# Transposing normalised rows and folded weights by VectorE turns and a round trip through memory, instead of on TensorE

## The chip, the cores and the metric

The kernel runs on one core of a Trainium2 chip. The metric is the time on the device of one execution, in microseconds (us). Before the change it is 2511.91 us, the median of 3 runs (2510.31 to 2513.71). All arithmetic is in fp32, except two small masks in bf16.

A core has five engines with a queue of instructions each: TensorE (PE in the profile, with its weight loads as PEld), VectorE (DVE), ScalarE (ACT), GpSimd (POOL), and SyncE (SP), which here only issues transfers between the on-chip memory and the chip's large memory.

## The reference

Four blocks run one after the other on `x` of 8 batch entries, 256 rows and 128 columns, with a context of 64 rows and 64 columns for each entry. The third block is nearly all of the time: six layers, each with self-attention, cross-attention to the context, and a feed-forward part. Cut to what matters:

```python
def _ln(x, g, b, eps=1e-05):
    m = jnp.mean(x, axis=-1, keepdims=True)
    v = jnp.mean(jnp.square(x - m), axis=-1, keepdims=True)
    return (x - m) / jnp.sqrt(v + eps) * g + b

def _mha(s, t, kv_w, q_w, o_w, o_b, mask):        # 16 heads of 64
    k, v = jnp.split(s @ kv_w, 2, axis=-1)
    q = t @ q_w
    k, v, q = (_heads(k), _heads(v), _heads(q))
    scores = jnp.einsum('bhqd,bhkd->bhqk', q, k) * D ** (-0.5)
    scores = jnp.where(mask[:, None] == 0, jnp.float32(-1000000000.0), scores)
    attn = jax.nn.softmax(scores, axis=-1)
    o = jnp.einsum('bhqk,bhkd->bhqd', attn, v)
    return o.transpose(0, 2, 1, 3).reshape(t.shape[0], t.shape[1], H * D) @ o_w + o_b
# each of 6 layers, t of (8, 256, 128):
#   n = _ln(t, norm);  t = t + _mha(n, n, sa_kv, sa_q, sa_ow, sa_ob, mask of 256 x 256)
#   n = _ln(t, norm);  t = t + _mha(context, n, ca_kv, ca_q, ca_ow, ca_ob, mask of 64)
#   n = _ln(t, pre);   t = t + relu(n @ ff_w1 + ff_b1) @ ff_w2 + ff_b2
```

## The kernel before

The whole of `t` stays on the chip, 128 rows in a partition group, two groups (`QT`) for each batch entry. A matmul contracts over partitions, so each of the three normalisations of a layer needs its result turned: from rows in partitions (`xn`) to the 128 columns in partitions (`tT`). That is done 3 x 8 x 6 = 144 times in the layers, by `ahead`.

The order of all work is written out by hand. Every step of every entry is put at a tick and a phase (`at(tick, phase, fn)`), the steps are sorted by that pair, and at the end a loop chains each engine's instructions in that order. An engine named in the tuple `engines` therefore runs its instructions in exactly this order: PE, DVE, ACT and POOL before the change. SP isn't in the tuple, so that its transfers go out when the framework places them.

A layer runs in three stages. Self-attention (SA) has four ticks for each entry `b`, with `T = T0 + 4b`. Cross-attention (CA) has two ticks for each, feed-forward (FF) one. Preparations for an entry lie some ticks before its own, so that stages overlap at their edges.

What one tick of SA does, by phase: two groups of scores on PE (1.0 and 1.1); their maxima on DVE and their exponentials on ACT (`exps`, phases 2.0 and 2.1, lines 905 to 921, eight ACTIVATE instructions for a tick); the division on POOL and the 32x32 turns of the weights on DVE (2.2, 2.3, 8.0, 8.1); the weighted values on PE (3.0); then, from phase 3.5, the projections of a later entry. For entry `b` the first key and both query projections (`project`, line 855) stand at tick T - 4, phases 3.5 to 3.7, the second keys at T - 3, the values at T - 2 and T - 1. Tick T - 4 of entry `b` is the first tick of entry `b - 1`, so for `b` from 1 to 7 these projections follow the scores of entry `b - 1` on PE. Each projection is copied out of PSUM by ACT.

`ahead` (line 802) makes `tT` in four steps. `moments` (DVE) and `scales` (POOL) find mean and reciprocal deviation. `normal` makes `xn`, on DVE for SA and on ACT for CA and FF. `trans` (line 837) turns `xn` with two PE transposes into PSUM, and ACT copies it into `tT` with the gain and the bias of the normalisation (line 843). SA has `trans` at (T - 5, 7.2): on ACT that lies ahead of the exponentials of tick T - 4. FF has it at (T - 1, 2.9), ahead of the relus of the same tick.

`plan_ca_weights` (line 1005) folds the cross-attention's weights, once in a layer: `turned` makes two transposes of a 128 x 1024 matrix, eight PE transposes and one ACT copy each, and `folded` multiplies the results into `AT` and `WVO`.

FF is `first` (line 1094; eight matmul records, then four relus on ACT) at tick T, and `second` (sixteen matmul records) at T + 1.

Of the kernel before, what the change touches and what calls it, by code (L numbers as in the profile page):

```python
# [8 lines left out]
F32 = mybir.dt.float32  # L9
I32 = mybir.dt.int32  # L10
BF16 = mybir.dt.bfloat16
AF = mybir.ActivationFunctionType
# [15 lines left out]
def tile_xattn_stack(ctx: ExitStack, tc: tile.TileContext, io, out: bass.AP):  # L28
    nc = tc.nc
# [21 lines left out]
    def tp_tile():  # L51
        return one_bank("tp")
# [56 lines left out]
    ident = const.tile([P, P], F32, tag="ident", name="ident")  # L109
# [83 lines left out]
    W = {}  # L193

    def load_sa(l):
        sk = sb([D, H * HD], "w_sk", 1, wpool)
        nc.sync.dma_start(out=sk, in_=io["L2_sa_kv"][l][:, : H * HD])

        sv = sb([D, 4, 2, 2 * HD], "w_sv", 1, wpool)
        sv_v = io["L2_sa_kv"][l][:, H * HD :].rearrange("p (g a x) -> p a g x", g=2, a=4)  # L200
        for a in range(4):
            nc.sync.dma_start(out=sv[:, a], in_=sv_v[:, a])
        sq = sb([D, H * HD], "w_sq", 1, wpool)
        nc.sync.dma_start(out=sq, in_=io["L2_sa_q"][l])
        sow = sb([P, HC, D], "w_sow", 1, wpool)
# [3 lines left out]
        W["sa", l] = (sk, sv, sq, sow, ob)  # L209

    def load_ca(l):

        ckv = sb([P, H * HD], "w_ckv", 1, wpool)
        for i in range(2):
            nc.sync.dma_start(
                out=ckv[DM * i : DM * i + DM],
                in_=io["L2_ca_kv"][l][:, H * HD * i : H * HD * (i + 1)],
            )
        cq = sb([D, H * HD], "w_cq", 1, wpool)
        nc.sync.dma_start(out=cq, in_=io["L2_ca_q"][l])  # L220
        cow = sb([P, HC, D], "w_cow", 1, wpool)
# [3 lines left out]
        W["ca", l] = (ckv, cq, cow, ob)  # L225

    def load_ff(l):
        w1 = sb([D, FF], "w_f1", 1, wpool)
# [50 lines left out]
    def at(tick, phase, fn):  # L279
        plan.setdefault(tick, []).append((phase, fn))  # L280
# [521 lines left out]
    def ahead(b, stats_at, normal_at, tT_at, g, bias, st, on_scalar=True):  # L802

        def moments():
            st["mv"] = sm([P, QT, 2], "mv")
            for j in range(QT):
                six = sm([P, 6], "six")
                nc.vector.bn_stats(six, tt(b)[:, j, :])
                nc.vector.bn_aggr(st["mv"][:, j, :], six)

        def scales():
            mv = st["mv"]
            ve = sm([P, QT], "ve")
            nc.gpsimd.tensor_scalar(ve, mv[:, :, 1], 1e-5, None, ALU.add)
            st["rstd"] = sm([P, QT], "rstd")
            nc.gpsimd.tensor_tensor(st["rstd"], ve, mhalf, ALU.pow)  # L816
            if on_scalar:
                nm = sm([P, QT], "nm")
                nc.gpsimd.tensor_tensor(nm, mv[:, :, 0], st["rstd"], ALU.mult)
                st["nm"] = sm([P, QT], "nm2")  # L820
                nc.gpsimd.tensor_scalar(st["nm"], nm, -1.0, None, ALU.mult)

        def normal():
            st["xn"] = sb([P, QT, D], "xn", 3)
            for j in range(QT):
                if on_scalar:
                    nc.scalar.activation(
                        st["xn"][:, j, :], tt(b)[:, j, :], AF.Identity,
                        scale=st["rstd"][:, j : j + 1], bias=st["nm"][:, j : j + 1],
                    )  # L830
                else:
                    nc.vector.tensor_scalar(
                        st["xn"][:, j, :], tt(b)[:, j, :], st["mv"][:, j, 0:1],
                        st["rstd"][:, j : j + 1], ALU.subtract, ALU.mult,
                    )

        def trans():
            ps = tp_tile()
            xn = st.pop("xn")
            for j in range(QT):  # L840
                nc.tensor.transpose(ps[:, j * P : (j + 1) * P], xn[:, j, :], ident)
            st["tT"] = sb([D, S], "tT", 3)
            nc.scalar.activation(st["tT"], ps[:, :S], AF.Identity, scale=g, bias=bias)

        at(*stats_at, moments)
        at(stats_at[0], 8.4, scales)
        at(*normal_at, normal)
        at(*tT_at, trans)

    def plan_sa(l, b, T):  # L850
# [134 lines left out]
        def mask():  # L985
            st["nm"] = load_mask(b)

        ahead(b, (T - 6, 8.3), (T - 5, 2.6), (T - 5, 7.2), norm_g, norm_b, st, False)
        at(T - 2, -1, mask)
        at(T - 4, 3.6, lambda: project(W["sa", l][2], "q", HD ** -0.5, 0, False))  # L990
        at(T - 4, 3.7, lambda: project(W["sa", l][2], "q", HD ** -0.5, 1, False))
# [13 lines left out]
    def plan_ca_weights(l, T):  # L1005


        st = {}
        W["fold", l] = st

        def turned(name, w, scale):
            def fn():
                ps = two_banks("tp")
                for c in range(HC):
                    nc.tensor.transpose(
                        ps[:, c * P : (c + 1) * P], w()[:, c * P : (c + 1) * P], ident
                    )
                st[name] = big("o", shape=(P, HC, P))
                flat = st[name].rearrange("p c x -> p (c x)")
                if scale is None:  # L1020
                    nc.scalar.copy(flat, ps)
                else:
                    nc.scalar.mul(flat, ps, scale)
            return fn

        def folded(name, cols, w):
            def fn():
                tiles = [two_banks("mm").rearrange("p (c d) -> p c d", c=HC) for _ in range(2)]
                res = sb([P, HC, D], name, 1, heap)
                for c in range(HC):  # L1030
                    for r in range(2):
                        rows = slice(r * HD, (r + 1) * HD)
                        nc.tensor.matmul(
                            tiles[r][rows, c, :], lhsT=st["kvT"][rows, c, cols],
                            rhs=w()[rows, c, :], start=True, stop=True,
                        )
                for r in range(2):
                    rows = slice(r * HD, (r + 1) * HD)
                    nc.scalar.copy(res[rows], tiles[r][rows])  # L1039
                st[name] = res  # L1040
            return fn

        at(T, 3.6, turned("kvT", lambda: W["ca", l][0], None))
        at(T + 1, 3.6, turned("WqT", lambda: W["ca", l][1], HD ** -0.5))
        at(T + 2, 3.6, folded("AT", slice(0, DM), lambda: st["WqT"]))
        at(T + 3, 3.6, folded("WVO", slice(DM, 2 * DM), lambda: W["ca", l][2]))

    keys_of = {}

    def plan_ca(l, b, T):  # L1050
        st = {}
# [25 lines left out]
        def res():  # L1077
            st["tb"] = residual(b, W["ca", l][3])

        ahead(b, (T - 4, 6), (T - 3, 2.95), (T - 2, 2.9), norm_g, norm_b, st)  # L1080
        if b % 2 == 0:
            at(T - 2, 3.7, keys_both)
        at(T + 2, 3.2, make_values)
# [11 lines left out]
    def plan_ff(l, b, T):  # L1095
# [29 lines left out]
                tt(b), ps[:, :S].rearrange("p (a d) -> p a d", a=QT), st["tb"]  # L1125
            )

        ahead(b, (T - 3, 6), (T - 2, 3.3), (T - 1, 2.9), pre_g[:, l : l + 1], pre_b[:, l : l + 1], st)
        at(T, 3.1, first)
        at(T + 1, 3.2, second)  # L1130

# [61 lines left out]
            at(T + n, 4.5 - 0.1 * n, step)  # L1193


    at(0, -1, lambda: load_sa(0))
    at(8, -1, lambda: load_ca(0))
    at(8, -0.9, lambda: load_ff(0))
    plan_start()
    for b in range(B):  # L1200
# [3 lines left out]
    for l in range(NL):  # L1204
        T_ca = T0 + 4 * B
        T_ff = T_ca + 2 * B
        for b in range(B):
            plan_sa(l, b, T0 + 4 * b)
        plan_ca_weights(l, T_ca - 6)
        for b in range(B):  # L1210
            plan_ca(l, b, T_ca + 2 * b)
            plan_ff(l, b, T_ff + b)
        if l > 0:
            at(T0, -1, lambda l=l: load_ff(l))
        if l + 1 < NL:
# [8 lines left out]
    for b in range(B):  # L1224
# [76 lines left out]
```

## Time and profile before

| | us |
|---|---|
| median of the runs | 2511.91 |
| the profiled execution, its own time | 2511.47 |
| its span, first to last instruction | 2509.8 |
| around the span | 1.7 |
| mean granted TensorE clock | 0.977 |
| DVE busy | 1821.0 |
| ACT busy | 1738.0 |
| POOL busy | 1442.8 |
| one layer, from the first weighted values after the fold to the same in the next (762.37 to 1147.80) | 385.4 |

One layer of 385 us is repeated six times; the two small blocks ahead take some 160 us, the last block is short. Busy shares say little for a kernel with three stages, since each has its own limit. Two further readings matter here. An engine's row in the timeline merges instructions of one line and tile, and a remark in brackets gives the idle time before it and who ended it. And the mean clock below 1 comes from short stretches in which the TensorE clock was granted at one half.

### The profile page before, as it was taken

How to read it: one execution, taken by the hardware profiler on the slowest of the kernel's cores; microseconds unless marked ns; L12 is line 12 of the kernel's file. 1: busy time of each engine (PE TensorE's matmuls, PEld its weight loads, DVE VectorE, ACT ScalarE, POOL GpSimd, SP SyncE). 2: the span in 40 equal slices, each digit the busy share in tenths (PEclk: the TensorE clock that was granted, in tenths of full speed). 3: DMA queues.
4: the chain of work that ended last, by engine and by line, in shares of the span. 5: the costliest groups of instructions: out<-in, count | busy, mean ns of one | idle time of the engine just before them, and what ended most of it. 6: DMA issues, size and time to landing. Idle time of an engine off the chain costs nothing.

```text
span 2509.8 us, 100205 instructions
## 1 busy us (share of the span) xinstructions
PE 2393.4 (95%) x42507; PEld 1766.2 (70%) x42507; DVE 1821.0 (73%) x5976; ACT 1738.0 (69%) x4540; POOL 1442.8 (57%) x2477
## 2 busy tenths in 40 slices
PE   8999999999999999999999999989999989999996
PEld 4667777677777676777776777776777776777774
DVE  5768887738887738887738887747887746888764
ACT  5567777667777657777657777657777657778651
POOL 3745557825556835556845555854555854555763
PEclk9999999999999999999999999999999999999996
DMA  6000021000011000012000012001002000000000
GB/s 172 2 11 17 22 57 34 3 11 20 20 47 52 2 12 20 20 37 63 2 8 23 20 29 63 11 3 27 21 20 70 12 2 20 20 20 12 2 1 17
DMA packets 94770, 64.31 MB, mean 26 GB/s; under 512 B 7729, under 2 KB 90353, under 8 KB 94322
## 3 DMA queue, kind: packets, MB, share of 16 engines
q1 hardware_dynamic: 93730, 57.57, 8.4%
q8 instruction: 334, 5.47, 0.9%
q14 instruction: 114, 0.93, 0.1%
q10 hardware_dynamic: 592, 0.33, 0.1%
HBM read 55.78 MB, written 2.10 MB: 23 GB/s over the span
## 4 chain that ended last, share of the span: by engine, by line
PE 69%; POOL 13%; DVE 7%; ACT 7%; issue 3%; POOLq 0%; DVEq 0%; ACTq 0%
PE mm L953 14%; PE mm L861 13%; PE sc L898 12%; PE mm L971 7%; PE mm L880 7%; POOL e L360 6%; PE mm L1103 3%; PE mm L1120 3%; DVE m L359 3%; POOL e L372 3%; PE mm L388 2%; ACT e L357 2%; ACT e L917 2%; PE sc L341 1%; POOL rstd L816 1%
## 5 line engine op out<-in xcount | busy, mean ns | idle before, releaser
L927 POOL TENSOR_SCALAR e<-e,rs 128x256 f32<-128x256 f32 x1536 | 702.5, 478 | 693.0 <-DVE rs L925 684.4
L917 ACT ACTIVATE e<-e,mn 128x256 f32<-128x256 f32 x1536 | 758.3, 495 | 131.3 <-DVE mn L912 130.5
L912 DVE CUSTOM_DVE_ANT_0 e<-sc,nm 128x256 f32<-128x256 f32 x1536 | 542.8, 419 | 124.3 <-PE sc L898 124.1
L937 DVE STREAM_TRANSPOSE eTc<-e 128x512 f32<-128x512 f32 x768 | 519.7, 697 | 66.2 <-POOL e L927 64.6
L953 PE MATMUL mm<-eTc,v 32*64 32x256 f32 x12288 | 383.4, 387 | 18.4 <-ACT AT L1039 8.1
L898 PE MATMUL sc<-k,q 64*32 64x256 f32 x12288 | 378.9, 380 | 5.9 <-DVE mn L912 4.2
L953 PEld LDWEIGHTS mm<-eTc,v 32*64 32x64 f32 x12288 | 285.0, 135 | 113.7 <-issue 30.2
L898 PEld LDWEIGHTS sc<-k,q 64*32 64x32 f32 x12288 | 220.5, 106 | 125.0 <-issue 46.1
L360 POOL TENSOR_TENSOR e<-e,m 128x1024 f32<-128x1024 f32 x112 | 213.1, 1902 | 129.2 <-DVE m L359 129.1
L917 ACT ACTIVATION_READ_ACCUMULATOR e<-e,mn 128x1 f32 x1536 | 287.2, 187 | 0.0
L359 DVE TENSOR_REDUCE m<-sc 128x16 f32<-128x1024 f32 x112 | 137.1, 1224 | 165.5 <-ACT e L357 165.5
L388 PE MATMUL mm<-v,k 128*128 128x128 f32 x1792 | 235.8, 287 | 5.4 <-DVE k L380 4.9
L388 PEld LDWEIGHTS mm<-v,k 128*128 128x128 f32 x1792 | 219.2, 200 | 26.5 <-issue 10.4
L341 PE MATMUL sc<-q,tT 128*32 128x256 f32 x3072 | 217.1, 382 | 0.0
L372 POOL TENSOR_TENSOR e<-e,r 128x1024 f32<-128x1024 f32 x112 | 213.0, 1902 | 0.7 <-DVE r L371 0.7
L366 ACT ACTIVATE e<-e 128x1024 f32<-128x1024 f32 x112 | 119.0, 1063 | 115.7 <-POOL e L360 115.7
L286 ACT COPY v<-mm 128x1024 f32<-128x1024 f32 x96 | 97.2, 1012 | 134.2 <-PE mm L880 134.2
L861 PE MATMUL mm<-tT,w_sk 128*128 128x256 f32 x768 | 189.6, 390 | 0.0
L971 PEld LDWEIGHTS mm<-w_sow,o 128*128 128x128 f32 x1536 | 175.1, 192 | 17.7 <-issue 14.4
L880 PE MATMUL mm<-w_sv,tT 128*32 128x256 f32 x3072 | 185.7, 382 | 0.0
L971 PE MATMUL mm<-w_sow,o 128*128 128x128 f32 x1536 | 183.6, 278 | 1.5 <-ACT WVO L1039 1.5
L861 PE MATMUL mm<-tT,w_sq 128*128 128x256 f32 x768 | 173.6, 379 | 0.0
(212 smaller groups left out, 3521.0 us busy)
## 6 DMA issues: line engine op xcount, KB each, us to landing
nm<-mask_d SPq DMA_DIRECT2D x192, 128.0 KB, 2.9
w_sk<-in_L_sa_kv_dram SPq DMA_DIRECT2D x6, 512.0 KB, 4.1
w_sv<-in_L_sa_kv_dram SPq DMA_DIRECT2D x24, 128.0 KB, 2.4
w_sq<-in_L_sa_q_dram SPq DMA_DIRECT2D x6, 512.0 KB, 3.5
w_sow<-in_L_sa_ow_dram SPq DMA_DIRECT2D x6, 512.0 KB, 4.0
w_ckv<-in_L_ca_kv_dram SPq DMA_DIRECT2D x12, 256.0 KB, 4.9
w_cq<-in_L_ca_q_dram SPq DMA_DIRECT2D x6, 512.0 KB, 4.9
w_cow<-in_L_ca_ow_dram SPq DMA_DIRECT2D x6, 512.0 KB, 3.9
```

The lines of the kernel that those rows point to most:

```text
L360: nc.gpsimd.tensor_tensor(e, e, m.unsqueeze(2).to_broadcast([P, 16, M]), ALU.subtract)
L372: nc.gpsimd.tensor_tensor(tl["e"], tl["e"], r.unsqueeze(2).to_broadcast([P, 16, M]), ALU.mult)
L388: nc.tensor.matmul(ps[:, :D], lhsT=eT[:, s].rearrange("p q x -> p (q x)"), rhs=vw[:, r, k, g, :], start=(s == 0), stop=(s == 7),)
L861: nc.tensor.matmul(ps[:, i * S : (i + 1) * S], lhsT=w[:, c * P : (c + 1) * P], rhs=st["tT"], start=True, stop=True,)
L880: nc.tensor.matmul(ps[32 * a : 32 * a + 32, i, :], lhsT=st["tT"][:, kb * 32 : (kb + 1) * 32], rhs=sv[:, a].rearrange("p g x -> p (g x)"), ...
L898: nc.tensor.matmul(sc[32 * a : 32 * a + 32, r, j, :], lhsT=st["q"][g][rows, a, qb * 32 : (qb + 1) * 32], rhs=st["k"][g][rows, a, :], start ...
L912: nc.vector.tensor_tensor_reduce(e[:, i, :], sc4[:, i, :], st["nm"][:, 2 * jj + i % 2, :], -1.0, 3.0 * BIG, ALU.add, ALU.min, mn[:, i : i ...
L917: nc.scalar.activation(e[:, i, :], e[:, i, :], AF.Exp, scale=-1.0, bias=mn[:, i : i + 1], accum_out=rs[:, i : i + 1],)
L927: nc.gpsimd.tensor_scalar(e[:, i, :], e[:, i, :], rs[:, i : i + 1], 1.0, ALU.mult, ALU.mult)
L937: nc.vector.transpose(eT[:, r, :, 2 * jj : 2 * jj + 2, :], e[:, 2 * r : 2 * r + 2, :].rearrange("p j (k x) -> p k j x", x=32),)
L953: nc.tensor.matmul(ops[a // 2][r * HD : (r + 1) * HD, a % 2, :S], lhsT=st["v"][kb // 4][rows, kb % 4, (2 * g + r) * HD : (2 * g + r + 1) * ...
L971: nc.tensor.matmul(st["ps"][:, j * D : (j + 1) * D], lhsT=st["oT"][c // 4][:, c % 4, j * P : (j + 1) * P], rhs=sow[:, c, :], start=(c == 0 ...
```

## The change

Three things change together.

First, `ahead` no longer uses PE. After `normal`, a new step `blocks` turns 32x32 blocks on DVE, and four transfers write the four block columns to a buffer in the large memory (`zd`). One tick later `fetch` reads the buffer back, so that the 128 columns lie in partitions (`raw`). `trans` is now one ACT instruction, from `raw` to `tT`, with the gain and the bias.

Second, the steps move. SA's statistics and normalisation go two ticks earlier for `b > 0`, and `trans` moves from (T - 5, 7.2) to (T - 4, 2.15); for `b = 0` it moves to (T - 4, 3.45). FF's normalisation goes one tick earlier and its `trans` from (T - 1, 2.9) to (T, 2.15). CA's normalisation goes two ticks earlier, its `trans` stays at (T - 2, 2.9).

Third, the two weight transposes are made in the same way, in place, with a regrouping copy on POOL, and the scale of the queries moves into `folded`. SP joins the engines whose order is fixed, and the weight loads are issued in parts over several ticks (`load_sa` and `load_ca` become generators, with a `yield` after each part).

```diff
+        def blocks():
+            xn = st.pop("xn")
+            z = sb([P, 4, QT, 32], "z", 2)
+            nc.vector.transpose(z, xn.rearrange("p q (j x) -> p j q x", x=32))
+            zd = st["zd"] = dram.tile([4, 32, 4, QT * 32], F32, tag="zd", name=uniq("zd"), bufs=4)
+            for j in range(4):
+                nc.sync.dma_start(
+                    out=zd[j].rearrange("b i x -> i b x"), in_=z[:, j].rearrange("p q x -> p (q x)")
+                )
+
+        def fetch():
+            st["raw"] = sb([P, 4, QT, 32], "raw", 4)
+            nc.sync.dma_start(
+                out=st["raw"].rearrange("p i q x -> p (i q x)"),
+                in_=st.pop("zd").rearrange("j b i x -> (j b) (i x)"),
+            )
+
         def trans():
-            ps = tp_tile()
-            xn = st.pop("xn")
-            for j in range(QT):
-                nc.tensor.transpose(ps[:, j * P : (j + 1) * P], xn[:, j, :], ident)
             st["tT"] = sb([D, S], "tT", 3)
-            nc.scalar.activation(st["tT"], ps[:, :S], AF.Identity, scale=g, bias=bias)
+            nc.scalar.activation(
+                st["tT"].rearrange("p (q i x) -> p q i x", q=QT, i=4),
+                st.pop("raw").rearrange("p i q x -> p q i x"), AF.Identity, scale=g, bias=bias,
+            )
...
         at(*normal_at, normal)
+        at(normal_at[0], normal_at[1] + 0.01, blocks)
+        at(normal_at[0] + 1, 0, fetch)
         at(*tT_at, trans)
...
-        ahead(b, (T - 6, 8.3), (T - 5, 2.6), (T - 5, 7.2), norm_g, norm_b, st, False)
+        if b == 0:
+            ahead(
+                b, (T - 6, 8.3), (T - 5, 2.6), (T - 4, 3.45), norm_g, norm_b, st, False
+            )
+        else:
+            ahead(b, (T - 8, 8.3), (T - 7, 2.6), (T - 4, 2.15), norm_g, norm_b, st, False)
...
+        for i in range(2):
+            at(T - 6 + i, 8.7, lambda i=i: turned(i))
+            at(T - 4 + i, -0.5, lambda i=i: fetched(i))
+        at(T + 1, 8.05, regrouped)
+        at(T + 2, 3.6, folded("AT", 0, lambda c: st[1][:, :, c, :], HD ** -0.5))
+        at(T + 3, 3.6, folded("WVO", 1, lambda c: W["ca", l][2][:, c, :]))
...
-        ahead(b, (T - 4, 6), (T - 3, 2.95), (T - 2, 2.9), norm_g, norm_b, st)
+        ahead(b, (T - 6, 6), (T - 5, 2.95), (T - 2, 2.9), norm_g, norm_b, st)
...
-        ahead(b, (T - 3, 6), (T - 2, 3.3), (T - 1, 2.9), pre_g[:, l : l + 1], pre_b[:, l : l + 1], st)
+        ahead(b, (T - 4, 6), (T - 3, 3.3), (T, 2.15), pre_g[:, l : l + 1], pre_b[:, l : l + 1], st)
...
-            at(T0, -1, lambda l=l: load_ff(l))
+            at(T0 + 3, -1, lambda l=l: load_ff(l))
         if l + 1 < NL:
-            at(T_ca + 4, -1, lambda l=l: load_sa(l + 1))
-            at(T_ff + 1, -1, lambda l=l: load_ca(l + 1))
+            by_parts(T_ca + 4, 2, load_sa(l + 1), 4)
+            by_parts(T_ff + 1, 1, load_ca(l + 1), 3)
...
-        mybir.EngineType.Pool,
+        mybir.EngineType.Pool, mybir.EngineType.SP,
```

The two new functions of `plan_ca_weights` that it calls do for a weight matrix what `blocks` and `fetch` do for a normalised entry: `turned(i)` makes one DVE transpose of 128 x 1024 and four transfers out, `fetched(i)` reads the matrix back over itself.

More of the change, by code (lines that the diff above doesn't have):

```diff
@@ L197, in load_sa @@
         nc.sync.dma_start(out=sk, in_=io["L2_sa_kv"][l][:, : H * HD])
+        yield
         sv = sb([D, 4, 2, 2 * HD], "w_sv", 1, wpool)
@@ L202, in load_sa @@
             nc.sync.dma_start(out=sv[:, a], in_=sv_v[:, a])
+        yield
         sq = sb([D, H * HD], "w_sq", 1, wpool)
         nc.sync.dma_start(out=sq, in_=io["L2_sa_q"][l])
+        yield
         sow = sb([P, HC, D], "w_sow", 1, wpool)
@@ L209, in load_sa @@
         W["sa", l] = (sk, sv, sq, sow, ob)
+        yield
     def load_ca(l):
@@ L218, in load_ca @@
             )
+        yield
         cq = sb([D, H * HD], "w_cq", 1, wpool)
         nc.sync.dma_start(out=cq, in_=io["L2_ca_q"][l])
+        yield
         cow = sb([P, HC, D], "w_cow", 1, wpool)
@@ L225, in load_ca @@
         W["ca", l] = (ckv, cq, cow, ob)
+        yield
     def load_ff(l):
@@ L1009, in plan_ca_weights, with turned, fetched, regrouped @@
         W["fold", l] = st
[L1011 to L1026, printed above, removed]
+        def turned(i):
+            w = W["ca", l][i]
+            z = big("o", shape=(P, 4, HC, 32))
+            nc.vector.transpose(z, w.rearrange("p (c j x) -> p j c x", j=4, x=32))
+            zd = dram.tile([4, 32, 4, HC * 32], F32, tag="wd", name=uniq("wd"), bufs=2)
+            for j in range(4):
+                nc.sync.dma_start(
+                    out=zd[j].rearrange("b i x -> i b x"),
+                    in_=z[:, j].rearrange("p c x -> p (c x)"),
+                )
+            W["cab", l, i] = zd
+        def fetched(i):
+            w = W["ca", l][i]
+            nc.sync.dma_start(out=w, in_=W.pop(("cab", l, i)).rearrange("j b i x -> (j b) (i x)"))
+            st[i] = w.rearrange("p (i c x) -> p i c x", i=4, x=32)
+        def regrouped():
+            st["kvT"] = big("o", shape=(P, HC, 4, 32))
+            nc.gpsimd.tensor_copy(st["kvT"].rearrange("p c i x -> p i c x"), st[0])
+        def folded(name, part, w, scale=None):
             def fn():
@@ L1033, in fn @@
                         nc.tensor.matmul(
-                            tiles[r][rows, c, :], lhsT=st["kvT"][rows, c, cols],
-                            rhs=w()[rows, c, :], start=True, stop=True,
+                            tiles[r][rows, c, :],
+                            lhsT=st["kvT"][rows, c, 2 * part : 2 * part + 2, :].rearrange(
+                                "p i x -> p (i x)"
+                            ),
+                            rhs=w(c)[rows], start=True, stop=True,
                         )
@@ L1038, in fn @@
                     rows = slice(r * HD, (r + 1) * HD)
-                    nc.scalar.copy(res[rows], tiles[r][rows])
+                    if scale is None:
+                        nc.scalar.copy(res[rows], tiles[r][rows])
+                    else:
+                        nc.scalar.mul(res[rows], tiles[r][rows], scale)
                 st[name] = res
             return fn
[L1043 to L1046, printed above, removed]
+        for i in range(2):
[4 more added lines that the diff above has]
+        at(T + 3, 3.6, folded("WVO", 1, lambda c: W["ca", l][2][:, c, :]))
     keys_of = {}
@@ L1193, in plan_l3, with by_parts @@
             at(T + n, 4.5 - 0.1 * n, step)
-    at(0, -1, lambda: load_sa(0))
-    at(8, -1, lambda: load_ca(0))
+    def by_parts(tick, step, load, n):
+        for i in range(n):
+            at(tick + i * step, -1, lambda: next(load))
+    by_parts(0, 1, load_sa(0), 4)
+    by_parts(6, 1, load_ca(0), 3)
     at(8, -0.9, lambda: load_ff(0))
```

## The prediction

> **What bounds the kernel now.** I read the busy times of the page first, then the groups by line, then the timelines of PE and ACT over one SA entry, then the stretches with the clock, and last the timelines of an FF stretch. The first line of the page's busy part:
>
> ```profile
> PE 2393.4 (95%) x42507; PEld 1766.2 (70%) x42507; DVE 1821.0 (73%) x5976; ACT 1738.0 (69%) x4540; POOL 1442.8 (57%) x2477
> ```
>
> PE is the bound: it is idle for 116 us of 2509.8. The group of the transposes to be removed (count, busy us, mean ns, idle before and who ended it):
>
> ```profile
> L841 PE MATMUL tp<-ident,xn 128*128 128x128 f32 x288 | 69.7, 307 | 39.9 <-ACT xn L827 33.4 <-DVE xn L832 2.8 <-DVE y L687 1.9
> ```
>
> So the change aims at the right engine. Whether PE can use the time depends on when `tT` is ready. One SA entry, PE (start, us, instruction) and then ACT:
>
> ```profile
> 988.85 0.44 PE L841 MATMUL tp<-ident,xn 128*128 128x128 f32 x2
> 989.22 1.96 PE L898 MATMUL sc<-k,q 64*32 64x256 f32 x64
> 991.10 1.99 PE L861 MATMUL mm<-tT,w_sk 128*128 128x256 f32 x8
> 992.93 3.62 PE L861 MATMUL mm<-tT,w_sq 128*128 128x256 f32 x16
> ```
>
> ```profile
> 989.89 0.57 ACT L843 ACTIVATE tT<-tp,L_norm_b,L_norm_g 128x256 f32<-128x256 f32 x1
> 990.94 0.51 ACT L917 ACTIVATE e<-e,mn 128x256 f32<-128x256 f32 x1 [0.48 <-DVE mn L912]
> ...
> 994.40 0.49 ACT L917 ACTIVATE e<-e,mn 128x256 f32<-128x256 f32 x1
> 994.80 0.18 ACT L917 ACTIVATION_READ_ACCUMULATOR e<-e,mn 128x1 f32 x1
> 994.89 0.99 ACT L286 COPY k<-mm 128x1024 f32<-128x1024 f32 x1
> ```
>
> The reader is to see three things. A pair of transposes holds PE for 0.37 us (988.85 to 989.22). `tT` is made at 989.89, just before the exponentials of the same tick, and is there when the key projection starts at 991.10. The exponentials end at 994.9, 3.8 us after that start, because they can't begin until the scores of their own tick have left PE.
>
> Stretches with busy us of PE, PEld, DVE, ACT, POOL, then clock and DMA:
>
> ```profile
> 989.22:1019.21 29.99, 29.99 (x643) 21.96 (x642) 25.42 (x98) 23.41 (x74) 16.24 (x36) 1.00 0.08 21
> ```
>
> ```profile
> 870.90:874.30 3.40, 0.79 (x8) 0.60 (x6) 2.80 (x4) 1.60 (x4) 3.07 (x7) 1.00 0.00 0
> 874.30:877.70 3.40, 3.40 (x15) 3.18 (x16) 2.93 (x8) 1.78 (x3) 3.30 (x3) 0.50 0.00 0
> 881.10:884.50 3.40, 1.55 (x12) 1.36 (x13) 1.16 (x2) 2.69 (x6) 3.06 (x7) 1.00 0.05 13
> 884.50:887.90 3.40, 3.40 (x13) 3.04 (x13) 0.29 (x1) 0.00 (x0) 0.15 (x1) 0.50 0.04 11
> ```
>
> An SA entry of 30.0 us has no idle PE at all, while DVE has 4.6 us to spare. And where PE was busy for under half of a 3.4 us stretch, the next one ran at half clock.
>
> [...]
>
> **SA, entries 1 to 7 of each layer.** `trans` goes to (T - 4, 2.15). The plan sorts by phase, and the eight exponentials of entry b - 1 in that tick have phases 2.0 and 2.1. ACT takes `trans` after them, about 994.9, and it takes 0.57 (the row L843; from memory on the chip rather than PSUM I take the same). `tT` is there at 995.5 in the old clock, the key projection was at 991.10: PE waits 4.4 us. Behind it in PE's order lie both query projections, the next scores and everything after, none of which may pass. Less the 0.37 of the pair, +4.0 an entry. The data itself comes early: `fetch` is two ticks (15 us) ahead, so the transfers aren't what is late here.
>
> Such a gap leaves at least one 3.4 us stretch with 2.2 us or more idle, so the next runs at half clock and loses half, 1.7 us (bounds: 0, if the half stretch falls into the wait; 3.4, for two in a row). I take 1.7. Together 5.7 x 7 x 6 = +239. In five layers the tick of entry 1's projection has the last `second` (1.9 us on PE) between scores and keys, which covers as much: -10. SA: +229.
>
> **FF.** `trans` at (T, 2.15) follows on ACT the relus and the next normalisation of the tick before, and any projection's copy. The old FF ticks:
>
> ```profile
> 897.63 1.89 PE L1103 MATMUL mm<-tT,w_f 128*128 128x256 f32 x8
> 899.36 1.95 PE L1120 MATMUL mm<-w_f,o 128*128 128x128 f32 x16
> 901.86 0.71 PE L841 MATMUL tp<-ident,xn 128*128 128x128 f32 x4 [0.55 <-DVE xn L832]
> 902.41 1.89 PE L1103 MATMUL mm<-tT,w_f 128*128 128x256 f32 x8
> ```
>
> ```profile
> 899.56 1.57 ACT L1108 ACTIVATE o<-mm,L_ff_b1T 128x256 f32<-128x256 f32 x4 [1.17 <-PE mm L1103]
> 901.00 0.89 ACT L827 ACTIVATE xn<-t,nm,rstd 128x128 f32<-128x128 f32 x2
> ...
> 911.31 1.02 ACT L867 ACTIVATE q<-mm 128x1024 f32<-128x1024 f32 x1 [0.70 <-PE mm L861]
> 912.23 0.56 ACT L843 ACTIVATE tT<-tp,L_pre_bT,L_pre_gT 128x256 f32<-128x256 f32 x1
> ```
>
> From one `first` to the next the new way is 1.75 (first) + 1.57 + 0.89 + 0.56 + 0.3 of hops = 5.1, against 4.8 before; PE's own work is 3.6, so it waits about 1.35 at three such ticks. In the last three, a projection's copy comes first: 1.0 + 0.56 + 0.15 = 1.7 us each, where the old `first` went on at once (it began at 911.33, beside the copy of 911.31). Entry 0 of the next layer is later still. Its statistics follow the `second` that ends at 896.8; old `xn` was there at about 901.9; a DVE turn of 128x256 is half of the 697 ns row of 128x512, 0.36. Then four stores at 0.45 us of SP each (the mask loads' spacing), landing about 1.8 to 2.4 us later (nearest rows: stores of the output 1.8, mask loads 2.9). SP's order puts `fetch` of FF entry 6 ahead, which waits for stores that are issued after these; then the load itself, 2.2, and ACT, 0.57. I come to 14.4 us after 896.8, where PE has 7.2 us of FF work and about 2.8 of waits above: PE waits 4.4 (3 to 7, by the landings), and one half-clock stretch adds 1.7. New extra time from the first `first` of a layer to the next SA scores: 1.35 x 3 + 1.7 x 3 + 4.4 + 1.7 = 15.3. Old: 50.1 us (878.06 to 928.20), of which 42.7 is matmul work by the row lengths, so 7.4 extra. +7.9, less 0.8 at the entry, where the wait of 2.61 us at 874.24 stays for the most part (the weighted values behind it need a DVE turn that begins at 874.02): +7.1, in five layers +36. The last layer has no entry 0 behind it: 0.
>
> **CA and weights.** CA's `trans` stands two ticks ahead of its reader, after no exponential that matters. Eight pairs at 0.28 to 0.58 with their waits, 0.45 on average: -3.6 a layer, -21. The 12 weight transposes took 1.02 us of PE each (746.22 to 747.24): -12; their DVE turns (1.4 us each) lie under SA's DVE slack.
>
> **What costs nothing.** 144 DVE turns at 0.36 are 52 us; in SA and CA (28.2 busy of 41.4) DVE has more to spare, and in CA the ACT result that the turn waits for is ready first. If that cover is gone, the scores' maxima queued behind the turn are late by as much, at most 0.36 an entry. Stores and loads add about 49 MB to 64, and the engines' share was 8.4%. SP's order binds only in FF, as counted; mask loads there are needed two ticks later.
>
> **Sum.** 2511.5 (the profiled execution: 2509.8 of span and 1.7 around) + 229 + 36 - 21 - 12 = 2743.5; the median shown is 0.4 above that execution. Forecast 2743. With no half clock and FF's low end: 168 - 10 + 28 - 33, so 2664. With two half stretches each and FF at +50: 2511 + 311 - 10 + 50 - 33, so about 2830.
>
> **Rivals.** *The wait without the clock*: the 4.4 us stand but fall so that PE's half-clock stretches lie in the waits, 2664. For it: a wait of 1.93 us in one layer wasn't followed by a half stretch; against: all stretches under half busy, as above, were. *Faster*: ACT makes `tT` before the exponentials of the tick, so that no wait takes the place of the transposes. Then PE gets back 53 (144 x 0.37), 40 of waits and 12 of weights, less FF's entry 0 (6.1 x 5) and some of the waits that other engines set: about 2440. For it: PE is 95% busy and the data is early. Against: the phases, and ACT in order. It decides below about 0.3 us of wait an entry. *Transfers late*: stores of 256-byte rows land much later than the rows above, SP backs up behind each `fetch`, and CA and FF wait too: at 2 us more for each of 96 entries with a half stretch in some, about 2950. Against: two or three ticks of slack.
>
> **How the numbers follow.** Chances: forecast 0.72, wait without the clock 0.12, faster 0.10, late transfers 0.06. The range 2630 to 2830 holds the first two but for their edges. The forecast's own range is 2664 to 2830. What this measurement can tell from no change is about 0.2%. Faster 0.10, same 0.02 (waits and gains cancel), slower 0.88.
>
> **What would show it.** Right: PE idle before L861 with `w_sk`, ended by ACT's `tT`, 42 times about 4.4 us; SA entries near 35.7 us; half clock in each; no wait of ACT on a transfer in SA. Wrong: the key projection following the scores at once; ACT waiting for `raw`; a mean clock that stays at 0.977.

## The result, and the profile after

The changed kernel took 2814.33 us (median of four runs, 2810.32 to 2821.06), the kernel before, run beside it, 2511.11 us (2509.0 to 2513.71). The ratio is 1.121, with a 95% interval of 1.1185 to 1.1234. The forecast was 2743, its range 2630 to 2830: slower, as predicted, and by 303 us where 232 had been worked out.

The busy times of the page after:

```profile
PE 2434.7 (87%) x42123; PEld 1791.0 (64%) x42123; DVE 1883.8 (67%) x6132; ACT 1742.8 (62%) x4528; POOL 1449.3 (52%) x2483
```

PE executes 384 instructions fewer than before (42507 less 42123: 288 transposes of entries and 96 of weights) and yet is busy 41 us longer, in a span that is 303 us longer (2813.0). Busy time that grows while the work shrinks points to a slower clock, and the mean granted clock did go from 0.977 to 0.941. What was withheld, the span times (1 less the clock), is 58 us before and 166 us after.

What PE waited for, from the view of waits (us in total, number of waits, longest), first after, then before:

```profile
PE mm L888 <- ACT tT L865: 202.4, 48, 6.3
PE mm L395 <- DVE k L387: 42.1, 48, 3.4
PE mm L1152 <- ACT tT L865: 41.6, 31, 1.6
```

```profile
PE tp L841 <- ACT xn L827: 33.4, 34, 2.6
...
PE mm L388 <- DVE k L380: 4.9, 6, 0.8
```

Before, the key projection never waited for `tT`. Now it waits at each of the 48 entries, 202 us in all, and `first` (L1152) waits for it at 31 of 48. And CA's weighted values (L388 before, L395 after) wait 42 us for the turned weights, where they waited 5 us: the waits for `xn` are gone, and another has come in their place.

One SA entry after, PE and then ACT (start, us, instruction, idle time before it):

```profile
1109.42 1.96 PE L925 MATMUL sc<-k,q 64*32 64x256 f32 x64
1115.73 3.78 PE L888 MATMUL mm<-tT,w_sk 128*128 128x256 f32 x8 [4.35 <-ACT tT L865]
1119.30 4.66 PE L888 MATMUL mm<-tT,w_sq 128*128 128x256 f32 x16
1123.89 1.96 PE L925 MATMUL sc<-k,q 64*32 64x256 f32 x64
```

```profile
1111.14 0.51 ACT L944 ACTIVATE e<-e,mn 128x256 f32<-128x256 f32 x1 [0.58 <-POOL e L954]
...
1114.60 0.49 ACT L944 ACTIVATE e<-e,mn 128x256 f32<-128x256 f32 x1
1115.00 0.19 ACT L944 ACTIVATION_READ_ACCUMULATOR e<-e,mn 128x1 f32 x1
1115.09 0.58 ACT L865 ACTIVATE tT<-raw,L_norm_b,L_norm_g 128x256 f32<-128x256 f32 x1
```

The scores leave PE at 1111.38. ACT works through the eight exponentials until 1115.09, and only then makes `tT`, with no remark in brackets: the data had long been there. The keys then take 3.78 us where they took 1.99. The same stretch in windows of 3.4 us (busy PE, PEld, DVE, ACT, POOL, then clock, DMA share, GB/s), and below it two stretches of about an entry each:

```profile
1109.00:1112.40 3.40, 2.37 (x76) 1.15 (x65) 2.61 (x13) 2.27 (x6) 2.09 (x5) 1.00 0.03 7
1112.40:1115.80 3.40, 0.07 (x1) 0.07 (x1) 2.52 (x13) 3.27 (x13) 0.97 (x3) 0.82 0.01 2
1115.80:1119.20 3.40, 3.40 (x8) 2.77 (x9) 2.14 (x6) 0.00 (x0) 3.23 (x8) 0.50 0.00 0
1119.20:1122.60 3.40, 3.40 (x12) 2.75 (x12) 0.00 (x0) 1.34 (x2) 0.38 (x1) 0.68 0.00 0
1122.60:1126.00 3.40, 3.40 (x79) 2.23 (x85) 0.91 (x5) 2.10 (x3) 0.00 (x0) 1.00 0.02 5
```

```profile
1115.73:1152.10 36.37, 32.48 (x640) 23.71 (x640) 25.70 (x98) 23.43 (x73) 15.78 (x35) 0.92 0.10 24
1152.10:1188.60 36.50, 31.68 (x641) 23.32 (x642) 26.42 (x100) 24.26 (x74) 17.24 (x39) 0.92 0.09 24
```

From the key projection at 1115.73 to the one two entries later, at 1188.06, it is 72.3 us: an entry takes 36.2 us instead of 30.0. Of the 6.2 more, 4.36 is the wait; with the 0.37 of the removed pair, 2.2 is left, and that is PE at half clock. Keys and queries lose 1.79 + 1.04 us to it in the first of the two entries, 1.45 in the second (keys of 3.44, queries of 3.62).

The windows also show how long it lasts. A mean clock of 0.82, 0.50 and 0.68 over 3.4 us each is 1.2, 3.4 and 2.2 us at one half: 6.8 us in all, of which 1.2 fell into the wait. I did the same for all entries, from the mean clock in the 15 us around each first key projection (that is exact to some 0.2 us):

| waits before the first keys | half clock for 6.8 us | for 3.4 us | none |
|---|---|---|---|
| entries 2 to 7, 36 waits of 3.8 to 5.0 us | 22 | 14 | 0 |
| entry 1, 6 waits of 2.3 to 2.9 us | 0 | 3 | 3 |

No other length occurs there. Keys and queries together (5.45 us at full clock) took 1.4 to 3.1 us more in the 36, 2.3 on average; over all 42 waits they lost 87 us, 2.1 a wait.

To see where the 303 us lie, I cut each layer by PE's timeline: SA from the first scores to the first mask matmul of CA, CA from there to the first `first`, FF from there to the next layer's first scores.

| | before | after | difference |
|---|---|---|---|
| SA, six layers | 1452.1 | 1690.6 | +238.5 |
| CA, six layers | 568.0 | 571.1 | +3.1 |
| FF, five layers | 247.4 | 303.3 | +55.9 |
| up to the first scores | 149.8 | 153.7 | +3.9 |
| from the last layer's first `first` to the end | 92.5 | 94.4 | +1.9 |

### The profile page after: what moved, and what is told of

It reads as the page before. It is cut to its first block, busy times and chain, and to the rows that moved or that the text cites. A ratio compares the mean times of both kernels' runs of the same rounds, so it can differ in the third digit from the quotient of the medians.

```text
span 2813.0 us, 100907 instructions
## 1 busy us (share of the span) xinstructions
PE 2434.7 (87%) x42123; PEld 1791.0 (64%) x42123; DVE 1883.8 (67%) x6132; ACT 1742.8 (62%) x4528; POOL 1449.3 (52%) x2483
## 4 chain that ended last, share of the span: by engine, by line
PE 51%; DVE 15%; ACT 14%; POOL 12%; issue 5%; DMA 1%; SPq 1%; DVEq 0%; POOLq 0%; ACTq 0%
PE mm L888 15%; PE sc L925 8%; ACT e L944 8%; PE mm L980 7%; PE mm L998 6%; POOL e L367 4%; DVE e L939 4%; PE mm L907 4%; POOL e L954 4%; DVE m L366 3%; ACT e L364 3%; PE mm L1152 3%; DVE eTc L964 2%; PE mm L395 2%; PE mm L1169 2%
## 5 line engine op out<-in xcount | busy, mean ns | idle before, releaser
L964 DVE STREAM_TRANSPOSE eTc<-e 128x512 f32<-128x512 f32 x768 | 513.8, 694 | 60.8 <-POOL e L954 60.1
L888 PE MATMUL mm<-tT,w_sk 128*128 128x256 f32 x768 | 263.4, 503 | 202.4 <-ACT tT L865 202.4
L888 PEld LDWEIGHTS mm<-tT,w_sk 128*128 128x128 f32 x768 | 183.6, 251 | 269.5 <-ACT tT L865 222.1
L925 PEld LDWEIGHTS sc<-k,q 64*32 64x32 f32 x12288 | 220.5, 106 | 143.9 <-issue 63.2
L395 PE MATMUL mm<-v,k 128*128 128x128 f32 x1792 | 234.1, 285 | 52.1 <-DVE k L387 42.1
L395 PEld LDWEIGHTS mm<-v,k 128*128 128x128 f32 x1792 | 213.9, 196 | 90.6 <-issue 42.9
L293 ACT COPY k<-mm 128x1024 f32<-128x1024 f32 x96 | 97.1, 1012 | 226.8 <-PE mm L888 226.8
L888 PE MATMUL mm<-tT,w_sq 128*128 128x256 f32 x768 | 200.0, 420 | 0.0
L373 ACT ACTIVATE e<-e 128x1024 f32<-128x1024 f32 x112 | 118.8, 1061 | 118.3 <-POOL e L367 118.3
L888 PEld LDWEIGHTS mm<-tT,w_sq 128*128 128x128 f32 x768 | 169.9, 221 | 31.7
```

The lines of the kernel that those rows point to most:

```text
L395: nc.tensor.matmul(ps[:, :D], lhsT=eT[:, s].rearrange("p q x -> p (q x)"), rhs=vw[:, r, k, g, :], start=(s == 0), stop=(s == 7),)
L888: nc.tensor.matmul(ps[:, i * S : (i + 1) * S], lhsT=w[:, c * P : (c + 1) * P], rhs=st["tT"], start=True, stop=True,)
L925: nc.tensor.matmul(sc[32 * a : 32 * a + 32, r, j, :], lhsT=st["q"][g][rows, a, qb * 32 : (qb + 1) * 32], rhs=st["k"][g][rows, a, :], start ...
L964: nc.vector.transpose(eT[:, r, :, 2 * jj : 2 * jj + 2, :], e[:, 2 * r : 2 * r + 2, :].rearrange("p j (k x) -> p k j x", x=32),)
```

## The experiments

Two theories stood for SA. A: the place of `trans` on ACT, behind the exponentials, makes the wait, and the transfers are early enough. B: the trip through memory, or the load that it puts on the other engines, makes the time.

**e1, the changed kernel with only SA's `trans` put ahead of the exponentials of its tick.**

```diff
-            ahead(b, (T - 8, 8.3), (T - 7, 2.6), (T - 4, 2.15), norm_g, norm_b, st, False)
+            ahead(b, (T - 8, 8.3), (T - 7, 2.6), (T - 4, 1.9), norm_g, norm_b, st, False)
```

> The changed kernel with one phase altered: SA's activation that makes the transposed rows for entries 1 to 7 stands ahead of the exponentials of its tick (phase 1.9) instead of behind them (2.15). Theory A (PE waits for the exponentials, and the half clock follows from that wait): the 4.36 us waits before the key projection vanish in 42 entries with their half-clock stretches, SA falls by about 250 us to just below the kernel before, total 2545 to 2580. Rival B (the extra time is the transfers, SP's fixed order and the added turns on VectorE, and the wait shown is only where it surfaces): the transposed rows are late wherever the activation stands, total stays above 2750.

Measured 2562.86 us (2562.09 to 2565.22), ratio 1.0224 (1.0205 to 1.0242), mean clock 0.973. ACT and PE of an SA entry in this kernel:

```profile
1010.20 0.60 ACT L865 ACTIVATE tT<-raw,L_norm_b,L_norm_g 128x256 f32<-128x256 f32 x1
1010.88 0.51 ACT L944 ACTIVATE e<-e,mn 128x256 f32<-128x256 f32 x1
```

```profile
1009.15 1.96 PE L925 MATMUL sc<-k,q 64*32 64x256 f32 x64
1011.04 1.99 PE L888 MATMUL mm<-tT,w_sk 128*128 128x256 f32 x8
1012.87 3.62 PE L888 MATMUL mm<-tT,w_sq 128*128 128x256 f32 x16
```

`tT` is there at 1010.80, the keys follow the scores at 1011.04 at full clock, and 251 of the 303 us are gone. All the turns, stores and loads are still in this kernel. That is A.

**e2, the kernel before, with PE's transposes where they were and only the ACT instruction that makes `tT` moved behind the exponentials.** No turn on DVE, no transfer is added.

```diff
+            st["tp"] = ps
+
+        def copied():
             st["tT"] = sb([D, S], "tT", 3)
-            nc.scalar.activation(st["tT"], ps[:, :S], AF.Identity, scale=g, bias=bias)
+            nc.scalar.activation(
+                st["tT"], st.pop("tp")[:, :S], AF.Identity, scale=g, bias=bias
+            )
...
         at(*tT_at, trans)
+        at(*(copy_at or (tT_at[0], tT_at[1] + 0.001)), copied)
...
-        ahead(b, (T - 6, 8.3), (T - 5, 2.6), (T - 5, 7.2), norm_g, norm_b, st, False)
+        ahead(b, (T - 6, 8.3), (T - 5, 2.6), (T - 5, 7.2), norm_g, norm_b, st, False, (T - 4, 2.15) if b else None)
```

> The kernel before, PE transposes kept at their place, with the activation out of PSUM alone moved behind the exponentials for entries 1 to 7 of SA; no turn on VectorE, no transfer, SP as before. Theory A: waits of about 4.4 us before the key projection and half-clock stretches as in the changed kernel, about +6.2 us for each of 42 entries, total 2740 to 2800; with the wait but no loss of clock it would be about 2690. Rival B: no difference from before, 2512.

Measured 2775.97 us (2767.94 to 2777.38), ratio 1.1064 (1.1041 to 1.1087), clock 0.940. PE's wait for `tT` in this kernel:

```profile
PE mm L867 <- ACT tT L846: 170.1, 42, 4.7
```

42 waits, one for each entry 1 to 7 of six layers, and 265 us more than before. The wait alone, in the kernel without a single new transfer, makes the loss, 6.3 us for each of the 42. With e1, the cause in SA is shown from both sides.

**e10, the changed kernel, with sixteen needless matmuls put into each wait** (b > 0), to tell the wait from the clock.

```diff
+        def warm():
+            ps = mm_tile()
+            for _ in range(16):
+                nc.tensor.matmul(ps[:, :P], lhsT=ident, rhs=ident, start=True, stop=True)
+
+        if b > 0:
+            at(T - 4, 3.45, warm)
```

> The changed kernel, with 16 needless 128x128 matmuls on PE (ident by ident into a PSUM tile that nobody reads) just ahead of the key projection of entries 1 to 7, inside the wait of 4.4 us, so that PE is busy there. Theory A (the loss is the wait plus a half clock that the idle PE brings on): the wait stays, its half-clock stretches go, the granted clock rises from 0.94 to about 0.97, total falls by 70 to 110 us to 2705 to 2745. Rival B (the half clock costs nothing, since other engines set the pace then): no fall, 2800 to 2830.

Measured 2745.03 us (2737.81 to 2746.41), ratio 1.0923 (1.0896 to 1.095), clock 0.973: 69 us less than the changed kernel, at the upper edge of what A expected. PE in this kernel (the trace has two records for each of the sixteen):

```profile
1112.51 1.96 PE L925 MATMUL sc<-k,q 64*32 64x256 f32 x64
1114.40 3.84 PE L1024 MATMUL mm<-ident 128*128 128x128 f32 x32
1118.83 1.99 PE L888 MATMUL mm<-tT,w_sk 128*128 128x256 f32 x8 [0.59 <-ACT tT L865]
```

The keys come as late as before (4.43 us after the scores), but take 1.99 us again, and so in all 42 entries. SA lost 79 us against the changed kernel (1611.3 by the same cut), 1.9 for each of 42 waits; the end of the kernel took 7.6 us more (see e3). So about a third of what the wait costs is the clock after it, and not the wait.

**e3, e1 with FF's `trans` back ahead of the relus of the tick before.**

```diff
-        ahead(b, (T - 4, 6), (T - 3, 3.3), (T, 2.15), pre_g[:, l : l + 1], pre_b[:, l : l + 1], st)
+        ahead(b, (T - 4, 6), (T - 3, 3.3), (T - 1, 2.9), pre_g[:, l : l + 1], pre_b[:, l : l + 1], st)
```

> The first experiment plus FF's activation back at (T - 1, 2.9). Theory A: the waits of 1.1 to 1.6 us before FF's first matmuls (7 us a layer in five layers) vanish, 25 to 40 us below the first experiment, about 2525. Rival B: the transfers of FF aren't there a tick earlier, so that the scalar engine waits for them and nothing is won, within 10 us of the first experiment.

Measured 2525.94 us (2521.8 to 2530.98), ratio 1.0074 (1.0053 to 1.0095): 37 us less than e1. FF went from 60 to 55 us a layer, and from the last layer's first `first` to the end it took 90 us instead of e1's 102. (The last block runs partly at half clock, from a point that differs between kernels: 61 us after that `first` the mean clock was 0.50 to 0.51 in the changed kernel and 1.00 until then, while in e1 it was 0.61 from 46 us on and 0.50 in the last 24; that is why the end took 94 us in the changed kernel and 102 in e1, with the same instructions. So most of the 12 us there may be the clock's, and the 23 us of the five FF stretches are what the move shows.) PE's waits at `first` fell from 41.3 us to 0.5: `trans` behind the relus was the same kind of fault. But B was right in part. ACT now waits for the transfer in FF too (27 waits for `raw` with 63.2 us together, where e1 has 9 with 24.9), and entry 0 behind it waits 7.8 to 9.3 us instead of e1's 5.6 to 6.1. With `trans` at its old place, FF's data is late.

**e4, e3 with the statistics and the normalisation of entry 0 one tick earlier,** since FF still held a wait for entry 0 of the next layer's SA.

```diff
-                b, (T - 6, 8.3), (T - 5, 2.6), (T - 4, 3.45), norm_g, norm_b, st, False
+                b, (T - 7, 8.3), (T - 6, 2.6), (T - 4, 3.45), norm_g, norm_b, st, False
```

> As the third, and entry 0 of SA normalised and stored one tick earlier (statistics at T - 7, normalisation at T - 6, read back at T - 5). Theory A: the wait of about 6 us with its half clock at the first key projection of five layers goes, 30 to 45 us below the third experiment, about 2485, below the kernel before. Rival B (the wait stands for a full SP queue that an earlier start doesn't empty): within 10 us of the third.

A miss: 2515.19 us (2509.07 to 2518.44), ratio 1.0024 (1.0012 to 1.0035), 11 us less than e3 and not 30 to 45, close to B. PE, ACT and SP's queue at that place in this kernel:

```profile
912.27 3.78 PE L888 MATMUL mm<-tT,w_sk 128*128 128x256 f32 x8 [6.85 <-ACT tT L865]
```

```profile
908.92 0.60 ACT L865 ACTIVATE tT<-raw,L_pre_bT,L_pre_gT 128x256 f32<-128x256 f32 x1 [5.29 <-DMA raw<-zd]
```

```profile
899.25 4.43 SPq L852 DMA_DIRECT2D zd<-z  x8
903.72 0.49 SPq L228 DMA_DIRECT2D w_cow<-in_L_ca_ow_dram  x1
904.31 0.69 SPq L230 DMA_DIRECT2D w_cob<-in_L_ca_ob_dram  x1
905.85 0.80 SPq L858 DMA_DIRECT2D raw<-zd  x2
```

ACT waits 5.3 us for a transfer, of an FF entry (`L_pre_gT`), and entry 0 stands behind it. SP has put out the eight stores of both entries in a row (4.43 us), then two weight loads, and both loads of `raw` at 905.85. Two causes were possible: the weight loads ahead, or the wait for the stores of the other entry.

**e7, e4 with the weight loads of CA five ticks later.**

```diff
-            by_parts(T_ff + 1, 1, load_ca(l + 1), 3)
+            by_parts(T_ff + 6, 1, load_ca(l + 1), 3)
```

> The fourth experiment with the loads of the next layer's cross-attention weights issued five ticks later (from T_ff + 6 instead of T_ff + 1). Theory A: entry 0's key projection still waits 6.9 us because SP's queue is full in FF (four stores of 0.54 us each and a wait for their landing for each entry, with 512 KB loads between them); without the loads the wait falls to about 3 us, 15 to 30 us below the fourth, about 2495. Rival B: the wait is set by the scalar engine and VectorE ahead of the stores, within 6 us of the fourth.

Measured 2510.7 us (2502.71 to 2517.63), ratio 1.0003 (0.9994 to 1.0012), 4.5 us less than e4: another miss for A, and within the 6 us of B. SP and PE:

```profile
896.96 4.40 SPq L852 DMA_DIRECT2D zd<-z  x8
903.63 0.81 SPq L858 DMA_DIRECT2D raw<-zd  x2
```

```profile
909.17 3.78 PE L888 MATMUL mm<-tT,w_sk 128*128 128x256 f32 x8 [6.04 <-ACT tT L865]
```

With no weight load between, SP still lets 2.3 us pass from the end of the stores (901.36) to the loads. So it is mostly the wait for the stores that binds, which A had named beside the loads; the weight loads are worth 0.8 us of PE's wait here (1.2 on average over five layers). Four of the eight stores are entry 0's, four an FF entry's. ACT waited for the FF entry's load first, so that load stands ahead in SP's order, and entry 0's behind it. e9 below tries them the other way round.

**e5, e4 with CA's exponential (L373) put behind the next tick's copy of the scores on ACT;** and **e6, the same in the kernel before.** CA's time hadn't changed with PE's work, so something else set it. A tick of CA in the changed kernel, ACT, DVE and POOL:

```profile
931.79 1.06 ACT L373 ACTIVATE e<-e 128x1024 f32<-128x1024 f32 x1 [0.98 <-POOL e L367]
932.75 0.99 ACT L364 COPY e<-sc 128x1024 f32<-128x1024 f32 x1
933.77 1.22 DVE L366 TENSOR_REDUCE m<-sc 128x16 f32<-128x1024 f32 x1 [1.20 <-ACT e L364]
935.08 1.90 POOL L367 TENSOR_TENSOR e<-e,m 128x1024 f32<-128x1024 f32 x1 [1.47 <-DVE m L366]
937.01 1.06 ACT L373 ACTIVATE e<-e 128x1024 f32<-128x1024 f32 x1 [1.22 <-POOL e L367]
```

Each row waits for the one above it. ACT copies the scores, DVE takes the maxima, POOL subtracts them, ACT takes the exponential, and only then, by its order, the next copy: 0.99 + 1.22 + 1.90 + 1.06, 5.2 us with the hops, a loop in which PE has no part. Not every tick is this short: the next three exponentials follow 6.1, 5.4 and 5.6 us apart, the first of them because POOL has a division and a residual's sum to do ahead of its subtraction. But four ticks take 22.4 to 22.6 us, before as after.

```diff
-        at(tick, 8, exps)
+        at(tick + 1, 2.05, exps)
```

> The fourth experiment, with CA's exponential on the scalar engine placed behind the next tick's copy of the scores out of PSUM (and so in the first block, which shares the function). Theory A: CA didn't gain from the removed transposes because a loop over three engines sets its tick (copy of the scores 1.0, maximum 1.2, subtraction 1.9, exponential 1.06, then the next copy, 5.3 us in all); with the exponential behind the next copy the loop is open and CA falls from 95 to about 90 us a layer, total 20 to 35 us below the fourth experiment, about 2487. Rival B: CA is bound by PE's own matmuls or by VectorE's added turns, no change, within 6 us of the fourth.

> The kernel before with the same move of CA's exponential alone. Theory A: PE's own work with the transposes nearly fills the tick of that loop there, so little is won, 2500 to 2512. Rival B: the loop is what limits CA before as well, and the move wins 20 us or more.

e5: 2482.35 us (2477.89 to 2482.87), ratio 0.9886 (0.9869 to 0.9902), 33 less than e4; CA went from 95 to 90 us a layer, and PE's wait for the turned weights from 42.1 us to 19.1. e6: 2492.36 us (2489.23 to 2497.76), ratio 0.9934 (0.9916 to 0.9951); CA went from 94.7 to 91.6. ACT in e5:

```profile
857.80 1.01 ACT L364 COPY e<-sc 128x1024 f32<-128x1024 f32 x1 [0.33 <-PE sc L355]
858.71 1.06 ACT L373 ACTIVATE e<-e 128x1024 f32<-128x1024 f32 x1
```

The copy now waits for PE's scores and the exponential for nothing, the reverse of the rows above: the loop is open. e6 came out between its two theories, nearer to B: the loop held the kernel before as well, but by 3.0 us a layer, where the changed kernel was held by 5.3 (95.2 in e4, 89.9 in e5). With the loop open in both, CA without PE's transposes is 1.7 us a layer shorter (91.6 in e6, 89.9 in e5): half of what I had forecast for their removal.

**e8, e7 with e5's edit, FF's normalisation one more tick earlier and the regrouping of the weights one tick earlier;** **e9, e8 with SA's `fetch` a little ahead of the FF entry's in SP's order.**

```diff
-        at(tick, 8, exps)
+        at(tick + 1, 2.05, exps)
...
-        at(T + 1, 8.05, regrouped)
+        at(T, 8.05, regrouped)
...
-        ahead(b, (T - 4, 6), (T - 3, 3.3), (T - 1, 2.9), pre_g[:, l : l + 1], pre_b[:, l : l + 1], st)
+        ahead(b, (T - 5, 6), (T - 4, 3.3), (T - 1, 2.9), pre_g[:, l : l + 1], pre_b[:, l : l + 1], st)
```

> The seventh with CA's exponential behind the next copy, FF's normalisation one tick earlier still, and the regrouping copy of the folded weights one tick earlier. Theory A: the gains add up, about 2455 to 2475, below the kernel before by 1.5% or more. Rival B: a further loop or queue takes up what is freed, 2490 to 2515.

```diff
-        at(normal_at[0] + 1, 0, fetch)
+        at(normal_at[0] + 1, 0 if on_scalar else -0.05, fetch)
```

> The eighth experiment with SA's load back from memory issued ahead of FF's of the same tick in SP's order. Theory A (entry 0's load waits on SP behind the stores of an FF entry): the wait of 3.2 us before the first key projection falls to about 1 us, total 8 to 18 us below the eighth, about 2461. Rival B (the load waits for its own stores): within 5 us of the eighth.

e8: 2474.42 us (2466.55 to 2475.3), ratio 0.9853 (0.9835 to 0.9871), 36 less than e7 and at the upper edge of what was expected. By the same cut CA gave 23 us of this and FF 20; CA took 91.5 us a layer and not e5's 89.9, so the gains didn't all add up. PE's longest wait before the keys fell from e7's 6.0 us to 3.3. e9: 2453.86 us (2452.5 to 2462.25), ratio 0.978 (0.9757 to 0.9803), a little below what was expected. Its busy times, and entry 0:

```profile
PE 2330.3 (95%) x42123; PEld 1722.3 (70%) x42123; DVE 1879.7 (77%) x6132; ACT 1730.1 (71%) x4528; POOL 1453.9 (59%) x2483
```

```profile
891.58 1.99 PE L888 MATMUL mm<-tT,w_sk 128*128 128x256 f32 x8 [1.36 <-ACT tT L865]
```

e9 computes all that the changed kernel computes, with as many instructions on PE, and beats both kernels: PE is busy 104 us less than in the changed kernel, and 63 less than before. The wait of 1.36 us is followed by keys at full clock. Of the 57 us that e9 gains on the kernel before, e6 shows that 19 are to be had there too, by the loop; some 38 are left for the turns through memory and what had to be moved with them. Against e6, by the same cut, FF has 22.9 us less, SA 14.6 and CA 3.9.

Not tried: the kernel before with its transposes left on PE and only the normalisations of CA and FF moved earlier. Its PE waited 33 us for `xn` there, so a part of the 38 may be had without any turn through memory; these runs can't tell how much. Nor was one store tried in place of the four of each entry, which, if it took SP the 0.54 us of one store now, would take 1.6 us (an estimate) off SP's work for an entry.

## Why the prediction was right, and where its size was off

| step | forecast | measured |
|---|---|---|
| SA and the weights in it | 229 - 12 = +217 | +238.5 |
| FF | +36 | +55.9 |
| CA | -21 | +3.1 |
| first block and last | 0 | +5.7 |
| sum | +232 | +303.2 |

The 71 us between the sums are three terms of much the same size: CA 24, SA 21.5, FF 20. The result lies close to the upper edge of the range, 2830, which had been worked out with two half stretches in every wait and FF at +50, and with CA's -21 in it. That the range still held is in part luck: CA's term was wrong, and the half stretches, two in about half of the waits, left room for it.

**SA: the mechanism and the wait, right.** Keys behind `tT` behind eight exponentials, 4.4 us forecast, 4.36 measured; 42 of them; entry 1 covered by the last `second`, which left 2.4 of wait by the forecast and 2.31 by the trace; no wait of ACT on a transfer in SA. e1 and e2 show that this is the cause. The term that was too small is the half clock: 1.7 us a wait, where keys and queries lost 2.1 on average. That a wait of 4.4 us brings it on was my estimate, from two stretches of the kernel before with PE busy for 0.79 and 1.55 of 3.40 us and a clock of 0.50 in the next. I had counted one half stretch of 3.4 us and none of it in the wait. In 22 of the 42 waits it was two, of which the first began in the wait; the bound of 3.4 that I had written for two stretches held. Times 42, 0.4 more is 16 us. A second term was too large: in e1, where the waits are gone, SA is 19.6 us below the kernel before, while the pairs (48 x 0.37) and the weights (12) would make 30. So some 10 us of the gain that the sum counted didn't come, in the pairs or in the weights; which of them, these runs don't tell.

**FF: the waits, right in sum by chance and wrong in place; the rest too small.** PE in the FF stretch of one layer after:

```profile
995.16 1.99 PE L1152 MATMUL mm<-tT,w_f 128*128 128x256 f32 x8 [1.12 <-ACT tT L865]
...
1010.09 3.78 PE L888 MATMUL mm<-tT,w_sk 128*128 128x256 f32 x8 [6.25 <-ACT tT L865]
1013.66 4.57 PE L888 MATMUL mm<-tT,w_sq 128*128 128x256 f32 x16
1019.83 1.99 PE L1152 MATMUL mm<-tT,w_f 128*128 128x256 f32 x8 [1.60 <-ACT tT L865]
```

The waits in this stretch are two of 1.12, one of 6.25, two of 1.60 and one of 1.63: 13.3 us, against 1.35 x 3 + 4.4 + 1.7 x 3 = 13.6. The ticks of FF itself wait less than I took, 7.1 us instead of 9.2. Entry 0 waits 1.9 longer (inside the 3 to 7 that I gave it; 5.9 us on average over the five layers): its stores took 0.54 us of SP each rather than 0.45, and ACT stood 5.02 us before the transfer. After it the keys and queries lose 1.8 + 0.95 = 2.7 us to the clock instead of 1.7 (2.0 on average). And at the entry of FF the changed kernel waits 1.53 us for the copy of CA's values (L316), which the sum hadn't. The remaining 2 or so are spread over rows that I didn't price.

**CA: the step that failed.** "CA's `trans` stands two ticks ahead of its reader, after no exponential that matters. Eight pairs at 0.28 to 0.58 with their waits, 0.45 on average: -3.6 a layer, -21." Where `trans` stands was right, but the step took PE as the bound of CA because PE was busy. The loop of ACT, DVE, POOL and ACT set the pace, so the time PE got back became its wait for the turned weights, 42 us instead of 5. e5 and e6 show it by opening the loop. The trace of before held the sign of it: ACT waited for POOL's subtraction ahead of the exponential and took the next copy straight after.

```profile
813.58 1.06 ACT L366 ACTIVATE e<-e 128x1024 f32<-128x1024 f32 x1 [0.95 <-POOL e L360]
814.54 0.99 ACT L357 COPY e<-sc 128x1024 f32<-128x1024 f32 x1
```

**The rivals.** *The wait without the clock* (2664) fell: the clock went down by 0.036, and e10 brings it back. *Transfers late* (2950) fell for SA and CA; in the change it holds at one place, entry 0 in FF, five waits of ACT with 23.4 us together, and with FF's `trans` a tick earlier, as in e3, for FF's own entries too. *Faster* (2440) fell for the change as it is. But with `trans` ahead of the exponentials and relus, and SP's order mended, the same idea gives 2453.86: the price I had put on it was close, but by luck: 19 us come from CA's loop, which I hadn't seen, and of what it counted for CA's pairs (48 x 0.37, 18 us) e9 has less than 4 against e6.

## What to carry to other kernels

ACT kept to its planned order here, so `tT` came after all that stood ahead of it there: behind eight exponentials it kept PE waiting for 4.36 us; ahead of them, in e1, it was there 0.24 us before the keys began. Before a step is moved, write down what will lie between its new place and its reader on that engine, and what that in turn waits for. In the changed kernel a wait of 4.4 us on PE cost another 2.3 us on average by the half clock that followed, while FF's waits of 1.0 to 1.6 us (30 of them) were followed by full clock, and those of 2.3 to 2.9 us went either way (entry 1: half clock after three of six). And a busy engine isn't a bound: PE was 95% busy before, and opening the loop of ACT, DVE and POOL alone took 19 us off (e6). So look for a loop of other engines with the same period before removing an engine's work.

## What the runs showed that I hadn't expected

After the same wait of 4.35 to 4.36 us half clock lasted either 3.4 us or 6.8 us, so what a wait cost in clock wasn't fixed; no run here shows what sets the length. Sixteen matmuls that compute nothing of use gave back 69 us (e10), so where a wait like this one can't be moved, work without use beside it can still pay. And SP, which only issues transfers here, came to bind at one place: four stores of a turned entry cost it 2.17 us, and the loads behind a store that it waited for went out 2.3 us after the last store in e7.
